# All four heads of two groups in eight turned by blocks, and row sums and routing ahead of the block transposes, in a post-norm decoder layer

## The chip, the cores and the metric

The kernel runs on one core of a Trainium2 chip. The metric is the device time of one execution in microseconds (us), the median of several runs. All data is float32. The engines are named as in the profile: PE does matrix products and transposes, PEld loads its weights, DVE, ACT and POOL work on vectors, and SP issues most DMA transfers. Each engine takes its instructions in the order in which they were written for it and waits on semaphores for the others.

## The reference

The layer takes `x` and `ctx` of shape 16 x 256 x 256 and a row of positions `frac` (16 x 256). It has three steps, each followed by a layer norm without weights. Cut to what matters here:

```
# 1. attention on fixed keys and values, 4 heads of 64
p = square(relu(q @ k.T)); x = norm(2*x + p @ v)

# 2. cross attention to ctx, 16 heads of 16, with a bias from positions
D      = clip(frac[:, None, :] - frac[:, :, None], -0.2, 0.2)
attn   = gamma * (Q @ K.T) / 4 + delta * (ap * max(D, 0) + an * min(D, 0))
probs  = softmax(attn, axis=-1)
x      = norm(x + (probs @ V) @ Wo.T + bo)

# 3. feed forward: the first of the largest of 8 gates chooses a low-rank addition
inner  = relu(x @ wi.T + wi_b + lora[top1](x))
x      = norm(x + inner @ wo.T + wo_b)
```

The change lies in step 2, in how `probs` is turned so that its key axis lies on the partitions, and in where parts of step 3 stand among it.

## The kernel before

Step 1 runs first, alone, to about 250 us. Then steps 2 and 3 run interleaved, in an order written out by hand (the whole program is under a manual schedule).

Step 2 is cut into 64 groups (`class Group`): one batch element and four of its heads, 256 queries by 256 keys. Group n belongs to batch element n // 4. The main loop at L1154 has one iteration per group and handles several at once: `now` is group n, `nxt` group n+1, `last` group n-1 and `older` group n-2. A group passes through these stages:

- `negative` (L636, POOL) and `positive` (L651, ACT) write the two halves of the position bias, the first into the tile `neg`, the second into four PSUM banks `ps_l`, one per head.
- `logits` (L659, PE) adds the products of queries and keys into the banks.
- `maxima` (L675, DVE) adds `neg` to the bank, keeps the sum in `neg` and takes each row's largest value.
- The rows are then made exponentials and turned, in one of two ways. In the first, `subtract` (L729, POOL or DVE) takes the maximum away, `turned` (L735, PE) transposes 128 x 128 pieces into PSUM, four per head, and `exps` (L749, ACT) writes their exponentials into the tile `pT`. In the second, `exp_rows` (L693, ACT) takes the exponential of the rows as they lie, with the maximum as bias, in two instructions per head; `blocks` (L701) transposes 32 x 32 blocks on DVE for two heads at once (into the tile `z`, or into the space of `kT`, which step 1 no longer needs) and writes them to DRAM (`away`); `fetch` (L722) reads them back by four DMAs, so that the blocks land in their places in `pT`.
- `attend` (L752, PE) multiplies `pT` by the values into the bank `av`, with a column of ones for the row sums. `keep` copies two groups' results out, and later pieces of the batch element (`gather`, `regroup`, `invert`, `spread`, `divide`, `project`) divide by the sums and apply the output weights.

Groups from number 14 on, but for the last two, are `direct` (L631): their heads 0 and 1 go the second way and their heads 2 and 3 the first.

Step 3 works on 512 tokens at a time, eight groups to such a block. Six of these blocks run inside the loop: with `part = (n - 15) % 8`, the iteration of part 0 transposes the block's rows (`turn`), part 1 computes the gates, part 2 chooses (`route`, a chain of small DVE instructions that ends in the tile `um`) and starts the inner product (`inner`, `turn_um`, `lora`), part 3 does its second half, and parts 4 to 7 do one quarter each of the outer product (`finish`, L994: `outer` on PE, then `add`, which adds the result to the rows on DVE and takes their statistics). In parts 5 and 7 the outer product uses the bank of the attends, and so no group is attended there; the group two before is attended one iteration later, together with the next one. So part 3's group is attended with part 4's in the iteration of part 6, and part 5's with part 6's in the next part 0.

In parts 2 and 3 (`halved`, L1215) the iteration has an order of its own. In the others, the block transposes of `now` are issued at L1302, after the row exponentials and ahead of `finish` (L1304); groups of parts 0 and 1 are `later` (L1210): their `blocks` and `fetch` wait for the next iteration. `fetch` of the other groups is issued at the start of the next iteration (L1189). All these DMAs go through SP's one queue, in order, together with those of the batch elements. PSUM space for transposes and small products comes from `tile_b`, three banks in turn.

Of the kernel before, what the change touches and what calls it, by code (L numbers as in the profile page):

```python
# [22 lines left out]
def tile_decoder_layer(ctx: ExitStack, tc: tile.TileContext, a: dict, out: bass.AP):  # L23
# [403 lines left out]
    if True:  # L427
# [199 lines left out]
        class Group:  # L627
            def __init__(self, batch, og):
                self.batch = batch
                self.o, self.i = divmod(og, 2)  # L630
                self.direct = DIRECT <= 4 * batch.b + og < 4 * B - 2  # L631

# [42 lines left out]
            def maxima(self):  # L675
# [3 lines left out]
                for g in range(4):  # L679
                    minus = self.direct and g < 2  # L680
                    for j in range(2):
# [10 lines left out]

            def exp_rows(self, g):  # L693

                for j in range(2):
                    nc.scalar.activation(  # L696
                        self.t[:, g, j, :], self.t[:, g, j, :], AF.Exp,
                        bias=self.mx[:, g, j : j + 1], scale=-1.0,
                    )

            def blocks(self):  # L701

                if self.i:
                    self.z = kT.rearrange("p n (c h q) -> p n c h q", c=2, q=32)
                else:
                    self.z = pm.tile([P, 4, 2, 4, 32], FP, tag="z", bufs=1, name="z")
                nc.vector.transpose(  # L707
                    self.z.rearrange("p n c h q -> p h c n q"),
                    self.t[:, 0:2].rearrange("p g j (c n k) -> p (g j) c n k", c=2, k=32),
                )  # L710
                self.away = drams.tile([P, 4, 4 * P // 2], FP, tag="blocks", name="away_z")
                nc.sync.dma_start(
                    out=self.away, in_=self.z.rearrange("p n c h q -> p n (c h q)")
                )

            def room(self):

                self.pT = pm.tile([P, 4, 2 * S], FP, tag="pT", name="pT")
                self.ps = {}
                self.pD = self.pT[:, 0:2].rearrange("p g (a c h q) -> p (g a) c h q", a=2, c=2, q=64)  # L720

            def fetch(self):  # L722
                for n in range(4):
                    nc.sync.dma_start(
                        out=self.pT[32 * n : 32 * n + 32, 0:2].rearrange("k g (a e) -> k (g a) e", a=2),
                        in_=self.away[:, n].rearrange("(r k) e -> k r e", k=32),
                    )

            def subtract(self, halves):  # L729
                for g, eng in ((2, nc.gpsimd),) if self.direct else zip((0, 2), halves):  # L730
                    rows = self.t[:, g : g + 2].rearrange("p g j k -> p (g j) k")
                    top = self.mx[:, g : g + 2].rearrange("p g j -> p (g j)").unsqueeze(2)
                    eng.tensor_tensor(rows, rows, top.to_broadcast([P, 4, S]), ALU.subtract)  # L733
# [18 lines left out]
            def attend(self):  # L752
# [4 lines left out]
                for k in range(2):  # L757
                    for g in range(4):
                        rhs = self.pT[:, g, k * S : (k + 1) * S]
                        to = batch.av[32 * g : 32 * g + 32, self.i * S : (self.i + 1) * S]  # L760
                        if self.direct and g < 2:
                            rhs = self.pD[:, :, k, g, :].rearrange("p r (j q) -> p j r q", j=2)
                            to = to.rearrange("p (j r q) -> p j r q", j=2, q=32)
# [18 lines left out]

        MADE, DIRECT = 5, 14
        batches = [Batch(b) for b in range(B)]
# [228 lines left out]
    with tc.manual_schedule():  # L1013
# [140 lines left out]
        for n in range(N + 2):  # L1154
# [53 lines left out]
            if now:  # L1208
                now.maxima()
                now.later = n >= FIRST and part in (0, 1)  # L1210
            if last and last.direct and last.later:
                last.blocks()
            if n == 29:
                by[NB] = scaling_of(rest_mv, newton(rest_mv, near_rest, 8), 8)
            if halved:  # L1215
                for g in range(2, 4) if last.direct else range(2):
                    last.turned(g)
                    last.exps(g)
                if part == 2:
                    ff.route()  # L1220
                if now.direct:
                    for g in range(2):
                        now.exp_rows(g)
                now.subtract((nc.gpsimd, nc.vector))
# [14 lines left out]
            else:  # L1239
# [7 lines left out]
                else:  # L1247
                    acts = "s0 s1 g s2 s3" if last.direct else "s0 e0 s1 e1 s2 s3"
                    if part != 0 or not ff:
                        acts += " x0 x1"  # L1250
                for act in acts.split():
# [9 lines left out]
                    elif act[0] == "x":  # L1261
                        if now:
                            now.exp_rows(g)
                    elif last:
# [17 lines left out]
            if ff and part == 0:  # L1282
# [3 lines left out]
                if now and now.direct:  # L1286
                    for g in range(2):
                        now.exp_rows(g)
            divided = batches[b - 2] if og == 0 and b >= 2 else None
# [9 lines left out]
            if done and not halved:  # L1299
                done.ready(newton(done.mv, done.near, 4))  # L1300
            if now and now.direct and not halved and not now.later:
                now.blocks()  # L1302
            if ff and part >= 4:
                ff.finish(part - 4, tile_v() if apart else None)  # L1304
            if last and (not last.direct or now and now.direct and not halved):
                for g in range(2, 4):
                    last.turned(g)
                    last.exps(g)
# [124 lines left out]
```

## Time and profile before

| what | value |
| --- | --- |
| median of 3 runs | 887.35 us (887.11 to 888.24) |
| the profiled execution | 887.49 us, its span 885.7 us |
| granted TensorE clock | 0.999 |
| DMA, over the span | 92.94 MB, 105 GB/s |
| L743, transposes on PE (heads turned the first way) | 640, 87.1 us busy, 277 ns each |
| L750, their exponentials on ACT | 160, 590 ns each |
| L696, exponentials of rows on ACT | 192, 498 ns each |
| L733, subtractions on POOL | 65, 1909 ns each |
| L707, block transposes on DVE | 24 into z at 1244 ns, 24 into kT at 1238 ns |
| DMA issues, blocks written to DRAM | 48 of 512 KB |
| DMA issues, blocks read back | 192 of 128 KB |

In a timeline, a line gives the start in us, the time in us, the engine, the source line, the operation, the tile written and the tiles read, the shapes, how many instructions were merged, and in brackets how long the engine sat idle before and what ended that. One float32 matmul shows as two records. Matmuls are pipelined: an instruction's own time is longer than the distance to the next, so eight transposes of 277 ns take about 1.04 us together.

### The profile page before, as it was taken

How to read it: one execution, taken by the hardware profiler on the slowest of the kernel's cores; microseconds unless marked ns; L12 is line 12 of the kernel's file. 1: busy time of each engine (PE TensorE's matmuls, PEld its weight loads, DVE VectorE, ACT ScalarE, POOL GpSimd, SP SyncE). 2: the span in 40 equal slices, each digit the busy share in tenths (PEclk: the TensorE clock that was granted, in tenths of full speed). 3: DMA queues.
4: the chain of work that ended last, by engine and by line, in shares of the span. 5: the costliest groups of instructions: out<-in, count | busy, mean ns of one | idle time of the engine just before them, and what ended most of it. 6: DMA issues, size and time to landing. Idle time of an engine off the chain costs nothing.

```text
span 885.7 us, 20853 instructions
## 1 busy us (share of the span) xinstructions
PE 862.4 (97%) x7708; PEld 513.1 (58%) x7708; DVE 693.3 (78%) x1975; ACT 577.0 (65%) x1012; POOL 466.6 (53%) x455
## 2 busy tenths in 40 slices
PE   8999999999999999999999999999999999999997
PEld 4334444444456776567547656754765675576655
DVE  6878899889779898769778877877887787777444
ACT  5766777777788788647747765774875577475111
POOL 1100223322479898656828765883976678374010
PEclk9999999999999999999999999999999999999999
DMA  5501101010001333454454536445453644642001
GB/s 139 159 1 43 54 24 44 31 49 1 8 8 48 99 98 110 139 162 149 158 155 150 158 129 184 151 155 168 138 164 133 193 151 135 181 149 102 28 7 41
DMA packets 70373, 92.94 MB, mean 105 GB/s; under 512 B 13824, under 2 KB 55296, under 8 KB 70272
## 3 DMA queue, kind: packets, MB, share of 16 engines
q1 hardware_dynamic: 69696, 91.35, 33.2%
q8 instruction: 61, 1.00, 0.5%
q14 instruction: 40, 0.33, 0.1%
q10 hardware_dynamic: 576, 0.26, 0.1%
HBM read 50.43 MB, written 39.58 MB: 102 GB/s over the span
## 4 chain that ended last, share of the span: by engine, by line
PE 44%; DVE 11%; issue 2%; POOL 1%; ACT 1%; DMA 0%; ACTq 0%; POOLq 0%; DVEq 0%
PE ps_l L945 9%; PE ps_b L978 6%; PE ps_l L664 5%; PE ps_v L764 5%; PE ps_b L743 4%; DVE neg L682 3%; PE ps_b L614 3%; PE ps_v L978 3%; PE ps_b L477 2%; PE ps_l L958 2%; DVE z L707 1%; PE ps_b L503 1%; PE ps_b L532 1%; POOL neg L733 1%; DVE dpos L547 1%
## 5 line engine op out<-in xcount | busy, mean ns | idle before, releaser
L682 DVE CUSTOM_DVE_ANT_0 neg<-ps_l,neg 128x256 f32<-128x256 f32 x512 | 181.5, 420 | 41.4 <-PE ps_l L664 38.3
L642 POOL TENSOR_SCALAR neg<-dneg,aneg,delta 128x512 f32<-128x512 f32 x252 | 198.9, 804 | 20.9 <-PE ps_b L743 10.0
L654 ACT ACTIVATE ps_l<-dpos,apos_d 128x512 f32<-128x512 f32 x256 | 172.2, 688 | 49.9 <-DVE mx L682 30.9
L354 DVE TENSOR_TENSOR pr<-pr 128x1024 f32<-128x1024 f32 x128 | 153.8, 1243 | 30.2 <-ACT pr L353 29.8
L733 POOL TENSOR_TENSOR neg<-neg,mx 128x1024 f32<-128x1024 f32 x65 | 124.0, 1909 | 85.4 <-DVE mx L682 84.3
L353 ACT ACTIVATE pr<-ps_a 128x1024 f32<-128x1024 f32 x128 | 125.0, 1026 | 53.0 <-PE ps_a L345 52.7
L345 PE MATMUL ps_a<-xnT,kT 64*64 64x512 f32 x1024 | 124.6, 593 | 1.0 <-ACT xnT L330 0.4
L364 PE MATMUL ps_v<-pr,vv 64*64 64x512 f32 x1024 | 122.7, 589 | 0.0
L945 PE MATMUL ps_l<-xt,wi 128*128 128x512 f32 x248 | 111.7, 596 | 0.2
L750 ACT ACTIVATE pT<-ps_b 128x512 f32<-128x512 f32 x160 | 87.4, 590 | 32.4 <-PE ps_b L743 30.9
L743 PE MATMUL ps_b<-ident,neg 128*128 128x128 f32 x640 | 87.1, 277 | 3.4 <-ACT pT L750 2.3
L743 PEld LDWEIGHTS ps_b<-ident,neg 128*128 128x128 f32 x640 | 71.5, 141 | 24.0 <-issue 6.2
L364 PEld LDWEIGHTS ps_v<-pr,vv 64*64 64x64 f32 x1024 | 45.0, 133 | 64.5 <-issue 54.6
L379 POOL TENSOR_TENSOR xt<-xt,half 128x512 f32<-128x512 f32 x15 | 19.1, 1274 | 119.8 <-ACT half L378 119.8
L419 POOL TENSOR_TENSOR hid<-hid,bo 128x256 f32<-128x256 f32 x32 | 43.6, 1366 | 71.8 <-ACT hid L251 71.8
L696 ACT ACTIVATE neg<-neg,mx 128x256 f32<-128x256 f32 x192 | 81.3, 498 | 0.0
L764 PE MATMUL ps_v<-pT,vaug 128*32 128x256 f32 x1024 | 74.3, 385 | 7.2 <-DVE x L991 6.0
L664 PE MATMUL ps_l<-kM,qT 32*64 32x256 f32 x2048 | 79.8, 388 | 0.0
L345 PEld LDWEIGHTS ps_a<-xnT,kT 64*64 64x64 f32 x1024 | 41.9, 133 | 65.3 <-issue 52.5
L945 PEld LDWEIGHTS ps_l<-xt,wi 128*128 128x128 f32 x248 | 45.6, 191 | 49.4 <-issue 44.6
L978 PE MATMUL ps_b<-wof,hT 128*128 128x256 f32 x304 | 68.4, 380 | 0.0
L524 POOL TENSOR_SCALAR kM<-keys,of_head 128x512 f32<-128x512 f32 x22 | 38.7, 1760 | 48.4 <-DVE keys L513 48.4
(137 smaller groups left out, 1183.3 us busy)
## 6 DMA issues: line engine op xcount, KB each, us to landing
pT<-away_z SPq DMA_DIRECT2D x192, 128.0 KB
away_z<-z SPq DMA_DIRECT2D x24, 512.0 KB
away_z<-kT SPq DMA_DIRECT2D x24, 512.0 KB
away_v<-raw SPq DMA_DIRECT2D x16, 512.0 KB
cT<-in_ctxT SPq DMA_DIRECT2D x16, 256.0 KB
v<-away_v SPq DMA_DIRECT2D x32, 128.0 KB
invs<-rows SPq DMA_DIRECT2D x16, 256.0 KB
x<-in_x SPq DMA_DIRECT2D x7, 512.0 KB
```

Of the source, the lines that this page charges most:

```text
L345: nc.tensor.matmul(sc[64 * k : 64 * k + 64, h, :], lhsT=kT[64 * h : 64 * h + 64, q, hf * P + 64 * k : hf * P + 64 * k + 64], rhs=self.xnT[ ...
L353: nc.scalar.activation(pr, sc, AF.Relu)
L354: nc.vector.tensor_tensor(pr, pr, pr, ALU.mult)
L364: nc.tensor.matmul(self.acc[k][64 * h : 64 * h + 64, :], lhsT=vv[64 * k : 64 * k + 64, hf, 64 * q : 64 * q + 64], rhs=pr[64 * k : 64 * k + ...
L642: nc.gpsimd.tensor_scalar(self.neg[:, g], self.batch.dneg, aneg[:, h : h + 1], delta, ALU.mult, ALU.mult,)
L654: nc.scalar.activation(banks[g], self.batch.dpos.rearrange("p j k -> p (j k)"), AF.Copy, scale=apos_d[:, h : h + 1],)
L664: nc.tensor.matmul(banks[g][64 * h : 64 * h + 64, j * S : (j + 1) * S], lhsT=self.batch.qT[rows, self.o, j * P + 64 * h : j * P + 64 * h + ...
L682: nc.vector.tensor_tensor_reduce(out=self.t[:, g, j, :], in0=banks[g][:, j * S : (j + 1) * S], in1=self.neg[:, g, j, :], scale=-1.0 if min ...
L733: eng.tensor_tensor(rows, rows, top.to_broadcast([P, 4, S]), ALU.subtract)
L743: nc.tensor.transpose(ps[:, k * S + j * P : k * S + (j + 1) * P], self.t[:, g, j, k * P : (k + 1) * P], ident,)
L945: nc.tensor.matmul(self.banks[g], lhsT=wi[:, c, f * P : (f + 1) * P], rhs=self.xT[:, c, :], start=(c == 0), stop=False,)
L978: nc.tensor.matmul(ps[:, 0:C], lhsT=self.hT[f][:, j * P : (j + 1) * P], rhs=wof[:, f, :], start=(f == 0), stop=(f == FC - 1),)
```

## The change

A direct group now has a number of pairs of heads that go the second way: 1 as before, or 2. It is 2 for groups of part 3 and part 4, from n = 18 to n = 58: eleven groups. Such a group has no `subtract`, no `turned` and no `exps`; `exp_rows` covers its four heads, `maxima` takes negative maxima for all four, `blocks` does two transposes (the first into `z`, the second into `kT`) and two writes, and `fetch` reads pieces of twice the size: four DMAs of 256 KB instead of 128 KB. In DRAM the blocks of the two pairs lie interleaved: a write of one pair goes to 512 runs of 1 KB instead of 128 runs of 4 KB, and a read takes runs of 2 KB instead of 1 KB.

Two orders change for all turns: `ff.route()` stands ahead of `last.blocks()` in part 2 (it stood inside the `halved` branch, after the transposes of the group before), and `ff.finish` stands ahead of `now.blocks()` in parts 4 to 7.

```
             def __init__(self, batch, og):
                 self.batch = batch
                 self.o, self.i = divmod(og, 2)
-                self.direct = DIRECT <= 4 * batch.b + og < 4 * B - 2
+                n = 4 * batch.b + og
+                self.direct = DIRECT <= n < 4 * B - 2
+                self.pairs = 0
+                if self.direct:
+                    self.pairs = 2 if DIRECT < n < 4 * B - 5 and (n - DIRECT - 1) % 8 in WHOLE else 1
...
-                    minus = self.direct and g < 2
+                    minus = g < 2 * self.pairs
...
-            def exp_rows(self, g):
-
-                for j in range(2):
...
+            def exp_rows(self):
+
+                for g in range(2 * self.pairs):
+                    for j in range(2):
...
             def blocks(self):
 
-                if self.i:
-                    self.z = kT.rearrange("p n (c h q) -> p n c h q", c=2, q=32)
-                else:
-                    self.z = pm.tile([P, 4, 2, 4, 32], FP, tag="z", bufs=1, name="z")
-                nc.vector.transpose(
-                    self.z.rearrange("p n c h q -> p h c n q"),
-                    self.t[:, 0:2].rearrange("p g j (c n k) -> p (g j) c n k", c=2, k=32),
+                self.away = drams.tile(
+                    [P, 4, self.pairs, 2 * P], FP, tag=f"blocks{self.pairs}", name="away_z"
                 )
-                self.away = drams.tile([P, 4, 4 * P // 2], FP, tag="blocks", name="away_z")
-                nc.sync.dma_start(
-                    out=self.away, in_=self.z.rearrange("p n c h q -> p n (c h q)")
-                )
+                for m in range(self.pairs):
+                    if m or self.pairs == 1 and self.i:
+                        z = kT.rearrange("p n (c h q) -> p n c h q", c=2, q=32)
+                    else:
+                        z = pm.tile([P, 4, 2, 4, 32], FP, tag="z", bufs=1, name="z")
+                    nc.vector.transpose(
+                        z.rearrange("p n c h q -> p h c n q"),
+                        self.t[:, 2 * m : 2 * m + 2].rearrange(
+                            "p g j (c n k) -> p (g j) c n k", c=2, k=32
+                        ),
+                    )
+                    nc.sync.dma_start(
+                        out=self.away[:, :, m], in_=z.rearrange("p n c h q -> p n (c h q)")
+                    )
...
             def fetch(self):
                 for n in range(4):
                     nc.sync.dma_start(
-                        out=self.pT[32 * n : 32 * n + 32, 0:2].rearrange("k g (a e) -> k (g a) e", a=2),
-                        in_=self.away[:, n].rearrange("(r k) e -> k r e", k=32),
+                        out=self.turned_in[32 * n : 32 * n + 32],
+                        in_=self.away[:, n].rearrange("(r k) m e -> k r (m e)", k=32),
                     )
 
             def subtract(self, halves):
-                for g, eng in ((2, nc.gpsimd),) if self.direct else zip((0, 2), halves):
+                for g, eng in ((2, nc.gpsimd),)[: 2 - self.pairs] if self.direct else zip((0, 2), halves):
...
-                        if self.direct and g < 2:
-                            rhs = self.pD[:, :, k, g, :].rearrange("p r (j q) -> p j r q", j=2)
+                        if g < 2 * self.pairs:
+                            rhs = self.pD[:, :, g // 2, k, g % 2, :].rearrange("p r (j q) -> p j r q", j=2)
...
-        MADE, DIRECT = 5, 14
+        MADE, DIRECT, WHOLE = 5, 14, (3, 4)
...
+            if ff and part == 2:
+                ff.route()
             if last and last.direct and last.later:
                 last.blocks()
...
-                if part == 2:
-                    ff.route()
...
+            if ff and part >= 4:
+                ff.finish(part - 4, tile_v() if apart else None)
             if now and now.direct and not halved and not now.later:
                 now.blocks()
-            if ff and part >= 4:
-                ff.finish(part - 4, tile_v() if apart else None)
             if last and (not last.direct or now and now.direct and not halved):
-                for g in range(2, 4):
+                for g in range(2 * max(last.pairs, 1), 4):
                     last.turned(g)
                     last.exps(g)
```

`room` lays out `pT` for one or two pairs (`turned_in`, `pD`) accordingly.

## The prediction

> **What bounds the kernel now.** I read the page first, then the timelines of all engines over one turn of eight groups, the DMA queue's waits, and the landing events of the transfers. Span first:
>
> ```profile
> span 885.7 us, 20853 instructions
> PE 862.4 (97%) x7708; PEld 513.1 (58%) x7708; DVE 693.3 (78%) x1975; ACT 577.0 (65%) x1012; POOL 466.6 (53%) x455
> ```
>
> PE is nearly always busy, so one would take PE work for the bound. The chain of waits repeats every eight groups; its L872 (the gates, part 1) starts at 509.39, 586.00, 662.62 and 739.24: one turn is 76.62 us, and there are six. I call the group at n = 15+8k "part 0", the next part 1, and so on, as the code's `part`. In the turn I read, the logits (L664) of parts 1 to 7 start at 583.09, 589.75, 604.28, 617.90, 627.16, 634.46, 643.63, and of the next part 0 at 650.93. PE from part 4 on:
>
> ```profile
> 622.26 3.62 PE L978 MATMUL ps_b<-wof,hT 128*128 128x256 f32 x16
> 625.72 1.04 PE L743 MATMUL ps_b<-ident,neg 128*128 128x128 f32 x8
> ...
> 633.50 1.04 PE L743 MATMUL ps_b<-ident,neg 128*128 128x128 f32 x8
> 634.46 1.12 PE L664 MATMUL ps_l<-kM,qT 32*64 32x256 f32 x32
> 635.51 1.93 PE L764 MATMUL ps_v<-pT,vaug 128*32 128x256 f32 x32
> 637.38 1.99 PE L614 MATMUL ps_b<-wo,oT 128*128 128x256 f32 x8
> 639.21 3.62 PE L978 MATMUL ps_b<-wof,hT 128*128 128x256 f32 x16
> 642.66 1.04 PE L743 MATMUL ps_b<-ident,neg 128*128 128x128 f32 x8
> ...
> 652.83 2.65 PE L764 MATMUL ps_v<-pT,vaug 128*32 128x256 f32 x32 [0.78 <-DVE x L991]
> ```
>
> The attends (L764) of part 0 show PE waiting: 0.78 us before them, and 2.65 us where the same 32 records at 635.51 took 1.93. So PE has about 1.6 us of slack there, and something else sets the end of that stretch. On DVE:
>
> ```profile
> 624.97 1.25 DVE L707 STREAM_TRANSPOSE kT<-neg 128x1024 f32<-128x1024 f32 x1 [0.72 <-ACT neg L696]
> 626.14 0.38 DVE L991 TENSOR_TENSOR x<-x,ps_b 128x256 f32<-128x256 f32 x1
> ...
> 633.75 1.25 DVE L707 STREAM_TRANSPOSE z<-neg 128x1024 f32<-128x1024 f32 x1 [1.91 <-ACT neg L696]
> ...
> 644.91 0.42 DVE L682 CUSTOM_DVE_ANT_0 neg<-ps_l,neg 128x256 f32<-128x256 f32 x1 [0.35 <-PE ps_l L664]
> ```
>
> From the maxima of part 7 (644.91) DVE runs without a gap through reciprocal, keys, dpos and the Newton steps to 651.2; ACT's x2 rows (651.34 to 653.32) and the exponentials (to 654.38) hang on that, and then the attend's end. So from 644.91 the turn is DVE then ACT; from part 0's attends to part 4 it is PE. What delays 644.91 delays the whole turn.
>
> **What the change does, part by part.** Eleven groups become "whole": parts 3 and 4 of the first five turns, part 3 of the sixth.
>
> PE loses 8 transposes in each: 1.04 us less the overlap, 0.97 to 1.04 (the L743 rows at 625.72 and 633.50). At part 2, routing stands ahead of the block transpose: PE now waits 0.53 us for `um` (the row at 597.83); routing takes DVE 594.98 to 598.19 = 3.21, and moved to 593.82 it is done at 597.03, before PE's L945 ends at 597.3, so the 0.53 goes. Routing's two PE transposes, now ahead of part 1's, need only the gates' copy of part 1. If nothing else bound, 11 × 1.04 + 6 × 0.53 = 14.6 us.
>
> POOL loses 11 subtractions of 1.9 us (off the path: it idled 7.34 before the one of part 3). ACT per whole group gains four exponentials (four take 1.69, so +1.6) and loses two L750 (1.08). DVE gains one transpose, 1.17 from start to start. SP gains one write, 0.33 to 0.41 to issue, on a queue that mostly waits.
>
> Costed at nothing, with the cover: in part 3 ACT idles 5.93 before L967 and DVE 2.40 before L971 (615.14), more than 1.6 and 1.17; were that cover gone, each would add what exceeds it. Part 3's attend comes only at part 6 (`apart` skips part 5), so its 1 MB fetch, issued near 618 to 620, has 14 us. Part 1's block, put 3.2 us later, is fetched only at 606.38 anyway: SP first waits there for the raw copy. Part 7's block goes behind the row sums, 1.06 later; its fetch landed at 659.67 and would land at 660.8; the attend at 660.83 waits for exponentials until 661.5. Less than 0.6 of cover is left; beyond that it costs one for one, and part 6's block and fetch, also later, have 1.5 left.
>
> Not hidden is part 4. By rows, in the same clock:
> 1. The outer product (L978) ended at 625.72; 0.53 earlier now: 625.19.
> 2. The row sums go first: add 0.26 later (the lag of L682 behind L664 at 584.14/584.40), 1.06 to the end of the statistics (626.14 to 627.20): 626.51. ACT's eight exponentials end at 625.98 (after the 0.53 shift, 622.78 + 8 × 0.40), so they do not bind.
> 3. Two transposes, 1.17 and 1.25: 628.93, where before it was 626.22. Part 5's maxima, queued behind them, start at 628.85 instead of 628.44; through L654 and the exponentials part 5's block comes at 634.2 and part 6's maxima at 635.3 (before: 635.91). No loss there.
> 4. SP writes the blocks, then fetches. Before:
>
> ```profile
> 626.24 0.33 SPq L712 DMA_DIRECT2D away_z<-kT  x1
> 629.22 1.80 SPq L724 DMA_DIRECT2D pT<-away_z  x4
> ```
>
> The write landed 2.85 after its issue and released the fetch 0.13 later; the fourth piece of the fetch landed at 633.60, 4.38 after the first issue; the attend of part 4, second half of the row at 635.51, read it at 636.45, with 2.85 of slack. Now the write is two DMAs whose DRAM side is 512 pieces of 1 KB, and the fetch is 1 MB, not 512 KB. Write: at least 2.62 (the commonest landing of the 4 KB form), at most 4.21 (a 512 KB out<-x in 1 KB pieces, at 810.35); I take 2.96 (the same store at 862.17, nothing beside it), the nearest in form. Fetch: at least 4.38 (half the bytes), at most 7.43 (eight pieces of 128 KB in part 3, 606.38 to 613.81, in a crowd); the four landings of 128 KB were 0.56 apart and issue allowed 0.46, so doubling the pieces costs up to four times 0.56 = 2.2 and no less than nothing. I take 1.0, a transfer partly issue-bound: 5.4. Landing: 628.95 + 2.96 + 0.13 + 5.4 = 637.4.
> 5. PE gets to this attend at 634.6 (logits at 632.6, held by L654; part 3's attend; 1.85 earlier than before). It then waits 2.8 us for DMA, a wait that was not there. Behind it on PE stand project (L614), the outer product, part 5's transposes and part 7's logits; for project DVE's `hid` waits, for the outer product its row sums, and for these, by the new order, part 6's block, and then part 7's maxima.
> 6. From landing L: attend L + 1.05, project 1.83, outer product 3.45, add 0.26, statistics 1.06, transpose 1.17: part 7's maxima start at L + 8.82. Before: 644.91. Each turn thus changes by L − 636.1: at 637.44, **+1.34**. If L came earlier, DVE's own queue would hold maxima at 643.8, a floor of −1.1.
>
> The sixth turn has no whole part 4, and there the new order helps:
>
> ```profile
> 788.23 1.93 PE L764 MATMUL ps_v<-pT,vaug 128*32 128x256 f32 x32 [1.63 <-DVE x L991]
> ```
>
> That 1.63 goes when the sums precede the block; with the 0.53 and 1.04 it could be 3.2, but part 4's one-pair block there goes behind the sums (626.51 to 627.7 in the clock above, 1.5 later), its fetch lands at 633.60 + 1.5 + 152.8 (the logits of part 5 are at 779.91) = 787.9, and that attend stood at 789.2, so 1.3 is sure; I take 1.6.
>
> Sum: 5 × 1.34 − 1.6 = +5.1. The profiled execution took 887.49 (span 885.7 and 1.8 around it), the median of runs 887.35; on the median this is **892.5 us**.
>
> [...] The trace has a 512 KB write at 2.62 and four 128 KB fetches at 4.38. [...]
>
> **Rivals.**
> *Fetch in time.* If L ≤ 635.0 the floor −1.1 holds in five turns: −5.5 − 1.6 gives 880.3; with DVE no bound at all, 14.6 gives 872.7. For it: PE's 97%. Against: write plus fetch would need 6.0 us, and the lowest rows sum to 7.1; only an earlier end of DVE's blocks could make it up.
> *A wash.* L between 636.1 and 636.8, the low ends of both rows: 0 to +0.7 a turn, −1.6 at the end: 885.8 to 889.1, say 887.5. The change then moves work from PE to the transfer and buys nothing.
> *The transfer is worse.* At both high ends L = 640.7, +4.6 a turn: 908.8; halfway between the taken and the high, +3: 901. It decides from L of 638.5. For it: DMA ran at 1.05 of its engines' time from 610 to 614 and out<-x there landed after 6.5 us, with part 3's second block now added. Against: from 627 the queue is nearly empty.
> That the change doesn't do what it says I exclude: in the built order the eleven groups have two block transposes each and eight transposes less on PE.
>
> **How the numbers follow.** Forecast (888.9 to 898, around 892.5) 0.42; transfer worse, 0.15; wash 0.15; fetch in time 0.28, because six of my links are lags of 0.2 to 0.5 and one unnoticed earlier release frees a us per turn. A change under 0.2% (1.8 us) can't be told from none here. Faster 0.28, same 0.15, slower 0.57. Range 881 to 902: half of the fast case and half of the worst case fall outside.
>
> **What would show it.** Right: in the first five turns PE idles 2 to 3 us before part 4's attend, the one x32 row after part 6's logits, released by pT's DMA; L743 is gone after parts 4's and 5's outer products; the 0.53 before `um` is gone; a turn lasts about 78 us, the sixth under 76. Wrong: attends of part 6 back to back and turns of 75.5; or the wait at part 0 (exponentials after the x2 rows) growing by itself.

## The result, and the profile after

The changed kernel takes 928.49 us in the median of four runs (925.08 to 930.47), the kernel before 887.31 beside it: a ratio of 1.0458, 95% interval 1.0426 to 1.049. It is slower, as forecast, but by 41.2 us and not by 5.1. The page of the changed kernel, whose profiled execution took 925.08 us:

```profile
span 923.3 us, 20672 instructions
PE 865.5 (94%) x7620; PEld 509.6 (55%) x7620; DVE 708.5 (77%) x1986; ACT 582.9 (63%) x1034; POOL 444.9 (48%) x444
...
PEclk9999999999999999989998999899899989999999
```

PE has 88 instructions less than before and is yet busy 3.1 us longer. The third line gives the granted clock in 40 slices: five slices in the interleaved part are below 9, one in each of the first five turns (a turn is eight groups). The PE timeline of one of them, from part 4's outer product on (start, duration, line; in brackets the idle time before and what ended it):

```profile
647.50 0.60 PE L464 MATMUL ps_b<-ident,hid 128*128 128x128 f32 x4
...
654.70 1.12 PE L668 MATMUL ps_l<-kM,qT 32*64 32x256 f32 x32
655.75 1.07 PE L779 MATMUL ps_v<-pT,vaug 128*32 128x256 f32 x16
663.38 1.94 PE L779 MATMUL ps_v<-pT,vaug 128*32 128x256 f32 x16 [6.56 <-DMA pT<-away_z]
665.24 2.54 PE L614 MATMUL ps_b<-wo,oT 128*128 128x256 f32 x8
667.62 3.62 PE L993 MATMUL ps_b<-wof,hT 128*128 128x256 f32 x16
...
691.08 1.07 PE L779 MATMUL ps_v<-pT,vaug 128*32 128x256 f32 x16 [1.74 <-DMA pT<-away_z]
```

The two rows of L779 at 655.75 and 663.38 are part 3's and part 4's attends: before, one row of 32 at 635.51 without a gap. Between them PE stands still for 6.56 us. The row behind the wait then takes 1.94 where the same 16 records take 1.07, and L614 takes 2.54 instead of 1.99. The last row is part 7's attend in the next part 1; it too waits now, 1.74 in this turn and 0.9 or less in the other four. The windows of the same turn, whose columns are length, busy time and count of PE, PEld, DVE, ACT and POOL, the granted clock, the DMA engines' share, and GB/s:

```profile
645.00:655.20 10.20, 10.03 (x93) 8.00 (x98) 7.95 (x27) 7.62 (x17) 7.21 (x8) 1.00 0.97 235
655.20:664.00 8.80, 2.24 (x48) 1.03 (x36) 4.62 (x20) 7.31 (x15) 8.14 (x9) 0.75 0.64 182
664.00:668.00 4.00, 4.00 (x25) 2.63 (x16) 0.87 (x2) 0.00 (x0) 0.00 (x0) 0.70 0.44 133
668.00:691.00 23.00, 20.97 (x212) 15.39 (x210) 18.08 (x65) 16.14 (x32) 15.98 (x16) 1.00 0.42 139
```

From 645 to 655, when part 4's write has to go out, the DMA engines are busy for 97% of the time. In the stretch of the wait and just behind it the clock is at 0.75 and 0.70: the clock's own record has 0.5 for 6.8 us there, from 2.75 us after the start of the wait to 3.02 after its end, and once in each of the other four turns for 6.8 to 10.2 us. The transfer itself, in the list of the chain that ended last (start, us, what):

```profile
644.21 3.45 PE ps_b L993 x16
651.09 4.40 DMA away_z<-kT
658.24 5.00 DMA pT<-away_z
```

The write lands 4.40 after its issue; the first piece of the fetch is issued at 655.64, the last at 658.24, and the last lands at 663.24, 12.15 after the write's issue.

Where the turn's time went, this turn (84.71 us from attend to attend of part 1, 606.37 to 691.08) against the same one before (76.62): to the end of part 4's outer product -0.45; from there to part 6's logits -1.54, for the two rows of eight transposes that are gone; part 6's attends +7.62, of which 6.56 is the wait; project to part 7's logits +0.55, since project begins at half the clock (L614's 2.54 for 1.99); part 7's attend +1.81; the rest +0.1. The sum is +8.09. The turns differ: from one start of the gates to the next, the first five are 6.1, 6.6, 8.7, 7.7 and 6.8 us longer than before (35.9 of the 37.6 us between the two profiled spans), and the sixth is 1.0 longer.

### The profile page after: what moved, and what is told of

Same layout as the page of the kernel before. It is cut to its first block, busy times and chain, and to the rows that moved or that the text cites. A ratio compares the mean times of both kernels' runs of the same rounds, so it can differ in the third digit from the quotient of the medians.

```text
span 923.3 us, 20672 instructions
## 1 busy us (share of the span) xinstructions
PE 865.5 (94%) x7620; PEld 509.6 (55%) x7620; DVE 708.5 (77%) x1986; ACT 582.9 (63%) x1034; POOL 444.9 (48%) x444
## 4 chain that ended last, share of the span: by engine, by line
PE 38%; DMA 9%; DVE 8%; issue 2%; SPq 2%; ACT 1%; DVEq 0%; ACTq 0%
PE ps_l L960 9%; PE ps_b L993 7%; DMA pT<-away_z 5%; PE ps_v L779 4%; PE ps_l L668 4%; PE ps_b L614 4%; DMA away_z<-kT 3%; PE ps_b L758 2%; DVE neg L686 2%; PE ps_l L973 2%; SPq L739 2%; PE ps_b L532 1%; DVE kT L716 1%; PE ps_b L503 1%; PE ps_b L477 1%
## 5 line engine op out<-in xcount | busy, mean ns | idle before, releaser
L748 POOL TENSOR_TENSOR neg<-neg,mx 128x1024 f32<-128x1024 f32 x54 | 103.1, 1910 | 46.9 <-DVE mx L686 40.2
L779 PE MATMUL ps_v<-pT,vaug 128*32 128x256 f32 x1024 | 79.8, 404 | 40.6 <-DMA pT<-away_z 36.9
L765 ACT ACTIVATE pT<-ps_b 128x512 f32<-128x512 f32 x138 | 75.6, 590 | 65.6 <-PE ps_b L758 62.5
L701 ACT ACTIVATE neg<-neg,mx 128x256 f32<-128x256 f32 x236 | 98.9, 498 | 0.0
L779 PEld LDWEIGHTS ps_v<-pT,vaug 128*32 128x32 f32 x1024 | 30.5, 112 | 88.6 <-issue 53.7
L758 PE MATMUL ps_b<-ident,neg 128*128 128x128 f32 x552 | 75.5, 277 | 3.0 <-ACT pT L765 2.3
L758 PEld LDWEIGHTS ps_b<-ident,neg 128*128 128x128 f32 x552 | 61.5, 141 | 20.4 <-issue 5.5
```

What stands on the lines that cost most here:

```text
L758: nc.tensor.transpose(ps[:, k * S + j * P : k * S + (j + 1) * P], self.t[:, g, j, k * P : (k + 1) * P], ident,)
L779: nc.tensor.matmul(to, lhsT=batch.va[:, k, self.head(g), :], rhs=rhs, start=(k == 0), stop=(k == 1),)
```

## The experiments

Each run was timed beside the kernel before (887.7 to 888.3 us in these comparisons).

**The orders alone.** No group is whole; both new orders stay.

```
-        MADE, DIRECT, WHOLE = 5, 14, (3, 4)
+        MADE, DIRECT, WHOLE = 5, 14, ()
```

> No group is whole here; only the two orders are changed (routing and row sums ahead of the block transposes). Theory (the loss is the wait of part 4's attend for the 1 MB of a whole group, and what follows on it): near the time before, 885 to 892 us, no PE idle of over 1.5 us before the attends of part 6, granted clock 0.998 or more; the wait before part 1's attend of part 7, whose block is 1.1 us later, may cost up to 1 us in each of six turns. Rival (the new orders make the loss, since all blocks of parts 4 to 7 start later): 905 us or more. The 0.53 before um should still be there if POOL's subtraction slows routing's L916 wherever it stands beside it.

897.68 us, ratio 1.0106 (1.0077 to 1.0134): the orders by themselves cost 9.4 us, more than the theory expected and less than its rival. Two later runs split them. The first keeps the new order of the routing alone, the second that of the row sums.

```
+            if now and now.direct and not halved and not now.later:
+                now.blocks()
             if ff and part >= 4:
                 ff.finish(part - 4, tile_v() if apart else None)
-            if now and now.direct and not halved and not now.later:
-                now.blocks()
```

> No whole groups, the old order in the finish, the routing of part 2 ahead of the block transposes (new). Theory: the row sums ahead of the transposes are what made 897.7 of the two orders, by part 7's later write, so the routing alone is worth between -2 and +1: 885 to 889. The rival, that the routing delays the transposes that stand behind it: 893 to 898.

> No whole groups, the old order in the routing, the row sums ahead of the block transposes at parts 4 to 7 (new). Theory: part 7's attend waits 1.4 to 1.9 us for its fetch in most turns, 895 to 899. The rival (routing): 886 to 889.

The routing: 888.17 us, 1.0001 (0.9992 to 1.0009). The row sums: 894.6 us, 1.0073 (1.0052 to 1.0095). So the loss is the row sums', as far as the runs can tell, and the routing moved nothing. PE's waits by line and releaser (us in all, times, longest), first the kernel before, then the row sums first:

```profile
PE ps_v L764 <- DVE x L991: 6.0, 6, 1.6
PE ps_b L919 <- DVE um L909: 2.6, 5, 0.5
```

```profile
PE ps_v L779 <- DMA pT<-away_z: 6.3, 7, 1.7
PE ps_v L779 <- issue: 3.6, 2, 2.0
```

The waits for the row sums' result (`x`) are gone but for one of 0.6, as they should be, and waits for the fetch have come in their place. ("issue" means that the profile shows nothing that released PE; the two waits stand at attends where the run with both orders waits for the fetch.) Waits for the last exponentials there grew too, from 0.4 to 3.2. Together PE's waits before attends grew from 6.9 to 13.7 us in the two profiled executions. One turn of that kernel, SP and then PE, shows why:

```profile
654.52 0.34 SPq L722 DMA_DIRECT2D away_z<-z  x1
657.92 1.74 SPq L739 DMA_DIRECT2D pT<-away_z  x4
...
663.54 1.07 PE L779 MATMUL ps_v<-pT,vaug 128*32 128x256 f32 x16 [1.68 <-DMA pT<-away_z]
```

Part 7's write stands behind its row sums: it is issued 7.34 ahead of the time at which PE could start this attend (663.54 less 1.68), before 8.26 (652.50 against 660.76). And the fetch is issued 3.40 after the write, where before that was 2.94 (652.50 to 655.44).

Why the routing brought nothing, in the DVE and POOL timeline of the changed kernel:

```profile
615.83 1.89 POOL L748 TENSOR_TENSOR neg<-neg,mx 128x1024 f32<-128x1024 f32 x1 [0.52 <-DVE lg L908]
616.04 1.73 DVE L916 TENSOR_TENSOR hot<-lg,top 128x32 f32<-128x32 f32 x1
```

and of the kernel before:

```profile
594.05 1.90 POOL L733 TENSOR_TENSOR neg<-neg,mx 128x1024 f32<-128x1024 f32 x1 [0.49 <-DVE mx L682]
595.39 0.60 DVE L901 TENSOR_TENSOR hot<-lg,top 128x32 f32<-128x32 f32 x1
```

The comparison of 32 columns takes 1.73 or 0.60, and in both kernels it ends 0.04 to 0.05 after POOL's subtraction does. The same in the run with the routing alone: POOL from 595.22 to 597.11, DVE to 597.16. Issued earlier, it only stands longer. Three pairs of ends are all that this rests on; what joins the two operations the traces do not show.

**The whole groups alone.** The old orders, parts 3 and 4 whole.

> Parts 3 and 4 are whole, both orders as before. Theory: part 4's second block ends about 1.4 us earlier (it still waits for eight exponentials), so the wait before its attend falls from 6.6 to about 5 us, and part 7's fetch is in time again: 905 to 915 us. Rival (the orders make the loss): under 895. Rival (the volume of DMA alone makes it, wherever the block stands): unchanged, 922 or more.

919.15 us, 1.0348 (1.0331 to 1.0365): 9.3 less than the changed kernel, which is again the price of the orders, but above the expected 905 to 915. The transfer is what makes most of the loss:

```profile
654.10 1.07 PE L779 MATMUL ps_v<-pT,vaug 128*32 128x256 f32 x16 [1.60 <-DVE x L1006]
659.87 1.93 PE L779 MATMUL ps_v<-pT,vaug 128*32 128x256 f32 x16 [4.70 <-DMA pT<-away_z]
```

**One of the two parts whole.** Part 3 with the old orders, then part 4 with the new ones.

```
-        MADE, DIRECT, WHOLE = 5, 14, (3, 4)
+        MADE, DIRECT, WHOLE = 5, 14, (3,)
```

> Only part 3 is whole, both orders as before. Theory: part 3's fetch has over 10 us until its attend at part 6, so nothing waits, PE loses 1.04 us in each of six turns and DVE's maxima of parts 5 to 7 move up with it: 880 to 884 us, faster than both kernels. Rival (more DMA traffic or DVE time costs in itself): 888 or more.

> Only part 4 is whole, both new orders. Theory (two causes: part 4's own second block and 1 MB, and part 3's 1 MB in the queue ahead of it): part 4's write lands in about 3 us instead of 3.6 to 5.1, the attend of part 4 still waits, about 4 us instead of 6.6: 908 to 918. Rival (part 4's own transfer is all of it): 923 or more. Rival (part 3 is all of it): under 900, as with the orders alone.

Part 3 alone: 887.1 us, 0.9986 (0.9977 to 0.9996), 0.1% less, where 880 to 884 was expected. Part 4 alone: 922.56 us, 1.04 (1.0377 to 1.0422), with waits of 4.5 to 5.2 before its attend in all five turns and long rows behind them (1.93 or 1.94 for 16 records in four turns, 1.51 for 12 in the other, where 12 take 1.06 elsewhere), at a mean granted clock of 0.978. Its second write landed after 3.65 to 3.86, not after the expected 3, and its fetch took 7.0 to 7.6, although no megabyte of part 3 runs ahead of it here. So part 4's own transfer makes most of the loss; part 3 as a whole group adds some 6 us more.

**The wait kept, the clock kept.** The changed kernel with 48 transposes of the identity on PE ahead of part 4's attend; nothing reads them.

```
                     groups[n - 3].attend()
+                if older.pairs == 2 and part == 6:
+                    ps = tile_b()
+                    for j in range(48):
+                        nc.tensor.transpose(ps[:, j % 4 * P : (j % 4 + 1) * P], ident, ident)
                 older.attend()
```

> The changed kernel with 48 transposes of the identity on PE ahead of part 4's attend where it is whole (five times), about 6.2 us of PE work that nothing reads. Theory (PE's idle lets the granted clock fall to half for some 7 us, and the attend and project after it run slower: 1.07 became 1.94 and 1.99 became 2.54): the clock stays at 1.0 there, about 1.4 us less in each of five turns, 919 to 924 us. Rival (the clock costs nothing, the wait alone does): 927 or more.

917.82 us, 1.0324 (1.0298 to 1.035): doing more work on PE makes the kernel 10.7 us faster. The PE timeline of that run:

```profile
648.21 5.46 PE L1203 MATMUL ps_b<-ident 128*128 128x128 f32 x48
654.79 1.07 PE L779 MATMUL ps_v<-pT,vaug 128*32 128x256 f32 x16 [1.12 <-DMA pT<-away_z]
655.79 1.99 PE L614 MATMUL ps_b<-wo,oT 128*128 128x256 f32 x8
```

The wait is as long as before (5.46 of filling and 1.12 of idling), but behind it the attend takes 1.07 and L614 1.99, as in the stretches where the clock's record is 1.0, and the mean granted clock is 0.996, the changed kernel's 0.979. PE's waits for the fetch sum to 9.6 in this run, and five fills of 5.46 make 27.3; together 36.9, the changed kernel's own total. So the transfer's lateness is not touched, and the 10.7 us are the clock's. They are more than the 1.4 a turn, 7 in all, that was expected from the turn shown. The record of the changed kernel agrees: of its five falls 3.0 to 6.2 us each lie behind the end of the wait, 23.7 in all, and at half speed that costs up to 11.9 us (an estimate).

**What makes the transfer late: four versions.** The write goes to runs of 1 KB (as in the change) or 4 KB (each pair of heads has its own area in DRAM); and the fetch waits for both writes as a whole, or its first half goes when the first write has landed. The second version:

```
-                    [P, 4, self.pairs, 2 * P], FP, tag=f"blocks{self.pairs}", name="away_z"
+                    [P, self.pairs, 4, 2 * P], FP, tag=f"blocks{self.pairs}", name="away_z"
...
-                for n in range(4):
-                    nc.sync.dma_start(
-                        out=self.turned_in[32 * n : 32 * n + 32],
-                        in_=self.away[:, n].rearrange("(r k) m e -> k r (m e)", k=32),
-                    )
+                for m in range(self.pairs):
+                    for n in range(4):
+                        nc.sync.dma_start(
+                            out=self.turned_in[32 * n : 32 * n + 32, :, 256 * m : 256 * m + 256],
+                            in_=self.away[:, m, n].rearrange("(r k) e -> k r e", k=32),
+                        )
```

> The changed kernel, but each pair of a whole group has its own part of DRAM: writes go in runs of 4 KB again, and the fetch is eight DMAs of 128 KB in runs of 1 KB. The bytes are the same. Theory (the write of part 4's second block takes 3.6 to 5.1 us because part 3's 1 MB fetch and the loads behind it still fill the queue): within 6 us of the changed kernel, 922 to 932. Rival (the 1 KB runs of the write make it long): the write falls to about 2.7 and the turn by 1 to 2 us, 917 to 922.

901.7 us, 1.0171 (1.0146 to 1.0196). The theory that part 3's megabyte makes the write long fell: the second write now lands after 2.8 us in four turns and 3.45 in one. But this run changed three things at once: the runs of the write, those of the read (1 KB instead of 2 KB), and the start of the fetch. Two more take them apart: the changed layout with the divided fetch, and this layout with the second pair fetched first, so that nothing can go before the second write is in.

```
-                for m in range(self.pairs):
+                for m in reversed(range(self.pairs)):
```

> The changed kernel, its store of the block transposes laid out as in it (runs of 1 KB in the write), but the fetch of each pair in eight transfers of 128 KB with runs of 1 KB, the first four of which need the first of the two writes alone. Theory W (the write's 1 KB runs are what made 928): the write still lands after 3.6 us or more, the last fetch after 11 us or more from the write's issue, 918 to 928. Theory R (the 2 KB reads, and that all of them waited for both writes): 899 to 908, the clock falling in at most two turns.

> The version with an area of its own for each pair (901.7), with the second pair's heads fetched first, so that nothing is fetched before the second write has landed. If the early start of the first half made the gain: 906 to 918, one wait of 4 us or more before part 4's attend, and the clock falls in most turns. If the length of the runs alone made it: 899 to 904.

| write's runs | fetch waits for both writes | first half goes with the first |
| --- | --- | --- |
| 1 KB | 928.49 (the change) | 909.68, 1.0238 (1.0213 to 1.0264) |
| 4 KB | 924.85, 1.0403 (1.0371 to 1.0434) | 901.7 |

(The read's runs are 2 KB in the first field and 1 KB in the others.) The last two expectations missed by their sizes: the early start of the first half is worth 18.8 or 23.2 us, the longer runs of the write only 3.6 or 8.0. The 18.8 and the 3.6 include the change of the read's runs, and the intervals of 928.49 and 924.85 overlap, so 3.6 is not clear of the scatter. The 23.2 includes that PE needs first the half that is fetched last there. Between the two versions of the right column only the layout in DRAM differs: with 1 KB runs the second write lands after 3.6 to 3.8. The fetch of the megabyte takes 6.7 to 8.1 in all three new versions. SP's and PE's timeline with both cures:

```profile
634.30 0.33 SPq L722 DMA_DIRECT2D away_z<-kT  x1
636.00 3.84 SPq L740 DMA_DIRECT2D pT<-away_z  x8
...
640.78 0.63 PE L780 MATMUL ps_v<-pT,vaug 128*32 128x256 f32 x4 [0.76 <-DMA pT<-away_z]
644.22 1.92 PE L780 MATMUL ps_v<-pT,vaug 128*32 128x256 f32 x12 [2.81 <-DMA pT<-away_z]
```

and with long runs but a late start:

```profile
648.20 0.33 SPq L722 DMA_DIRECT2D away_z<-kT  x1
651.16 4.50 SPq L740 DMA_DIRECT2D pT<-away_z  x8
...
658.65 2.15 PE L780 MATMUL ps_v<-pT,vaug 128*32 128x256 f32 x16 [4.72 <-DMA pT<-away_z]
```

In the first, the fetch begins 1.70 after the second write's issue, in the second 2.96 after it. The first has two shorter waits with work between them, and the rows behind are long in one turn of five, the one shown (1.92 for the 12 records, 1.06 in the other four); the second has one long wait, and the 16 records behind it take 2.14 or 2.15 in all five.

**Making part 3 alone pay.** Part 3's megabyte and the next loads of `cT` and `frow` stand on SP ahead of part 4's write of one pair, which then landed after 4.2 to 6.05 us instead of 2.6 to 2.85. Here part 4's loads are held back to the end of part 5:

```
             for extra in pieces(n)[2]:
-                if extra:
+                if extra and n > FIRST and (n - FIRST) % 8 == 4:
+                    held.append(extra)
+                elif extra:
                     extra()
...
+            while held and (n - FIRST) % 8 == 5:
+                held.pop(0)()
```

> Only part 3 whole, old orders, and the two loads of a later batch element (384 KB) that stand on SP between part 3's fetch and part 4's write go to the end of part 5's iteration. Theory (in the kernel with part 3 whole, part 4's 512 KB write takes 4.5 to 6.0 us where it took 2.6 before, since the queue holds part 3's 1 MB and these loads; its attend then waits 1.2 us): the write falls below 4 us, the wait goes, about 1 us less in each of five turns: 880 to 885. Rival (part 3's 1 MB alone fills the queue): 886 to 889, unchanged.

883.59 us, 0.9959 (0.9944 to 0.9973): 0.4% faster than the kernel before, which is small but clear of the scatter. The place of the loads is worth some 3 of these 4.3 us, going by the run without it: part 4's write now lands after 2.6 to 4.4. (The profiled execution was the slowest of the six, 886.81, with one wait of 2.66 left.) Two other edits brought nothing. The first is part 3 whole, without the late loads, with the row sums first in the sixth turn alone:

> Only part 3 whole, old orders, but in the sixth turn the row sums stand ahead of the block transposes. Theory (in the sixth turn no query product stands behind part 5's logits, PE waits over 1.6 us for part 5's row sums, and the clock then falls to half for 3.4 us): the wait and the half clock there go, 1.5 to 2.5 us less than with part 3 whole alone: 884 to 886. Rival (the sixth turn's attend then waits for DMA or DVE instead): no change, 887.

887.05 us, 0.9996 (0.998 to 1.0013): the rival's value; in the sixth turn the attend now waits 1.58 for the fetch. The second is the late loads with an area for each pair:

> Only part 3 whole, old orders, late loads of part 4 (883.6), with an area of its own for each pair of heads and fetches of 128 KB: 881 to 884 if part 3's long-run transfer also clears the way for part 4's write of one pair; unchanged, 883 to 885, if part 3's transfer was hidden in any case.

883.39 us, 0.9954 (0.994 to 0.9968): not to be told from 883.59; part 3's transfer was hidden.

**Can both parts pay?** Old orders, both cures of the transfer, late loads; then the same with the row sums first in part 4, or between the two transposes, or first in part 5.

> Parts 3 and 4 as whole groups, with the old order in the finish and the routing, an area of its own for each pair and fetches of 128 KB, and part 4's next loads held back to the end of part 5's: 886 to 893 if the transfer is what made 919 of the old orders and its cure is worth what it was in the changed kernel (901.7 less some 9 for the orders, less 4 for the loads). A rival: the old order issues the write later, so the waits stay above 3 us and the clock falls again: above 900. Below 883 only if part 4's first product block costs less than its wait.

> As the version with both parts whole, old orders, areas of their own and late loads (892.3), but with the row sums ahead of both transposes in part 4 alone. The waits for the row sums' result there (1.6 to 2.1 us in six places) go; the writes are issued some 1.8 us later, and the fetch, which was in time in all but two turns, is then late by what slack it lacked: 886 to 893; above 893 if it had no slack at all and the clock falls with the wait.

> As that version (892.3), but with the row sums between the two transposes in parts 3 and 4: the row sums wait for one transpose, as in the kernel before, so the waits of 1.6 to 2.1 us for their result go; the first half's write is not moved, the second is issued some 1 us later: 880 to 887. The rival, that the second half then lands late: 889 to 894.

> As the version with both parts whole, old orders, areas of their own and late loads (892.3), but with the row sums ahead of the transpose in part 5 alone, where VectorE stands idle for 1.9 us before that transpose and TensorE waits 1.5 to 2.1 us for the sum, six times, 10.5 in all. If that wait is the price that is left: 882 to 887, and no wait of more than 0.3 us for the row sums' result before part 4's attend. If the fetch is late right behind it: 888 to 893.

In this order: 892.3 us, 1.0048 (1.0036 to 1.006); 899.32, 1.0126 (1.011 to 1.0142); 892.88, 1.0042 (1.0027 to 1.0057); 892.2, 1.0037 (1.0018 to 1.0056). None is faster than before. The two in the middle were aimed at a wait that does not arise in part 4: in the first of the four versions PE's timeline has it at 563.88, where the attends of parts 3 and 4 need the bank that part 5's row sums read. (Why the second version is 7 us slower than the first stays open.) The last run moved just those row sums, and PE's waits show what became of it, first without the move, then with it:

```profile
PE ps_v L780 <- DVE x L1007: 14.5, 11, 2.1
PE ps_v L780 <- DMA pT<-away_z: 4.7, 3, 2.3
```

```profile
PE ps_v L780 <- DMA pT<-away_z: 13.0, 10, 2.9
PE ps_v L780 <- DVE x L1007: 4.3, 5, 1.1
```

10.2 us of waits for the sums went, 8.3 came back as waits for the fetch, and the time did not move. The transfer stood right behind, as the run's rival said.

## Why the prediction was too low

The place and the wait were right: PE waits before part 4's attend for the DMA of `pT` in each of five turns, and the rivals "a wash" and "fetch in time" are both out. The rival "the transfer is worse" comes nearest, but even its upper end, 908.8, is 20 below. Two steps failed: step 4, the length of the transfer, was too short by 3.7 us a turn, and the clock's fall behind the wait was missing from step 6. Step by step, in the turn read above:

1. *The outer product of part 4 ends 0.53 earlier, since the `um` gap goes.* Wrong: the gap before the row at 619.61 is still 0.52 (1.11 in two other turns), as one of routing's operations ends with POOL's subtraction in both orders (0.04 to 0.05 after it). The step took routing's 3.21 us as a fixed length; that operation went from 0.60 to 1.73 when moved. The run with this order alone: 888.17, no change. (The 0.45 that the turn shown does gain up to here lies in its first attend, which takes 1.35 to the next row instead of 1.79.)
2. and 3. *Row sums, then two transposes, 3.74 us.* Right. In the DVE timeline:

```profile
647.70 0.42 DVE L1006 TENSOR_TENSOR x<-x,ps_b 128x256 f32<-128x256 f32 x1 [1.67 <-PE ps_b L993]
...
648.71 1.23 DVE L716 STREAM_TRANSPOSE z<-neg 128x1024 f32<-128x1024 f32 x1
649.86 1.20 DVE L716 STREAM_TRANSPOSE kT<-neg 128x1024 f32<-128x1024 f32 x1
```

From the outer product's end at 647.50 to the second transpose's end at 651.06 it is 3.56.

4. *Write 2.96, release 0.13, fetch 5.4: 8.49 in all.* This is the step that failed. It measured 4.40 + 0.14 + 7.60, and 12.15 from issue to landing. In the five turns the write took 3.6 to 5.1 and the fetch 7.2 to 7.6, in part beyond the high ends (4.21 and 7.43). The value chosen for the write was that of a store with "nothing beside it", and "from 627 the queue is nearly empty" was read from the kernel before, where the DMA engines were busy for 36% of the stretch from 625 to 634. In the changed kernel they are busy for 97% from 645 to 655, with part 3's own megabyte, fetched from 642.35 to 650.07, and the loads. But that traffic is not most of the error: with part 4 alone whole the write still took 3.65 to 3.86 and the fetch 7.0 to 7.6. For the write the runs of 1 KB count, since runs of 4 KB bring it to 2.8 in four turns of five; the traffic may explain the two turns with 4.40 and 5.08. The doubled fetch was priced at +1.0, and it costs 3.2 over the old 4.38: its four pieces of 256 KB land 1.2 to 1.6 apart, where those of 128 KB landed 0.56 apart. Part 5's write of 512 KB, issued at 658.77 while the fetch runs, may lengthen it; no run separates that. And the structure went unseen: with one fetch for both pairs, half of the data waits for a write that it does not need. Letting that half go early is worth 18.8 to 23.2 us in the four versions, the clock's part included. With 12.15 for the 8.49 the prediction's own sum would give +5.0 a turn and 910.8 in all (an estimate); the rest of the way to 928.49 lies in what follows.
5. *PE waits 2.8.* 6.56 here, 5.8 to 6.7 in the five turns: the 2.8 plus the 3.7 of step 4.
6. *From the landing on, 8.82 to part 7's maxima, each turn +1.34.* This failed too: the stretch was costed at full clock. PE idles 6.56, the clock's record falls to 0.5 at 2.75 into that wait, and PE pays on the work behind it: 10.7 us in all by the run with the fill, a term that no step had.

*Costed at nothing: part 7's block, with 0.6 of cover.* Wrong too: the write and the fetch of part 7 land later than the step added up, as its row sums put both of them behind, and the attend waits 1.74 in the turn shown. With the row sums' order alone the cost is 6.5 us, with both orders 9.4; whether these differ by more than the runs scatter stays open, as their intervals overlap.

*Sixth turn, -1.6.* It did not come: the 1.63 for `x` at the attend is gone, and in its place PE waits 1.77 for part 4's fetch there. That turn is 1.0 us longer than before.

The terms, as far as runs separate them: of 41.2 us, the cures of the transfer (first half early, long runs) give back 26.8, and with it nearly all of the clock's 10.7; the orders are 9.4; some 5 are left, which is what both parts whole with old orders and all cures still cost (892.3 against 887.7). That remainder did not go in any of three further versions, and its cause stays open. The saved PE work is real (1.54 in this turn), but it only shortens PE's way to a wait for a transfer that cannot come sooner.

## What to carry to other kernels

A round trip by DRAM must be priced for its own size and length of runs and in the traffic of the changed kernel, not from a transfer of half the size in the gap that the old one left (8.49 was taken here, 12.15 measured); ask for each piece of the fetch which write it really needs, and let it go with that. A wait on PE can have a second price: behind the waits of 5.8 to 6.7 us here the clock's record stayed at 0.5 for 3.0 to 6.2, and it shows as longer rows of the same instruction (1.94 for 1.07); without it the kernel was 10.7 us faster. And an order that removes a wait for one result delays every transfer that is issued behind it: with the row sums first, in parts 4 to 7 or in part 5 alone, waits for the sums became waits for a fetch.

## What the runs showed of the hardware

The clock. In the changed kernel the record of 0.5 begins 2.3 to 5.1 us after the start of PE's waits of 5.8 to 6.7 us, still inside them, and lasts 6.83 us in four turns and 10.24 in one; between these five it stands at 1.0 for 75.09 us twice and 78.51 twice. All these lengths are within 0.01 of whole multiples of 3.413, a third of the 10.24. Shorter waits were not safe, going by the rows right behind them. Where the record is 1.0, the 16 records of an attend take 1.07 and L614 takes 1.99. Behind a wait of 2.66, in the version with part 3 whole and late loads, the 16 took 1.94; behind one of 2.92 in the last run, 1.73; behind one of 2.00 in the run with both orders, 1.50, and L614 then 3.21. Others near 2 us passed: behind one of 1.98, in the run with the row sums first, it was 1.07 and 1.99. In the version with the row sums first in part 4, two waits of 2.11 had 32 records of 4.07 and 3.82 behind them, and a third of 2.11 had 20 of 1.49, the same as a wait of 1.60 in the version with the row sums between the transposes. Behind 1.86 and 1.80, with both orders, the 16 took 1.07. Of two waits close together, 1.45 and 1.65 in the version with 1 KB runs and the first half early were followed by 1.92 for 12 records, 1.66 and 1.75 in another of its turns by 1.06. So these runs give no one length of wait that divides the two.

SP's issue. The four pieces of part 4's fetch take SP 3.03 us in the turn shown, 2.58 in the last and some 1.75 in the other three; two of them were issued 1.75 apart (656.02 and 657.77), beside a packet of 1.40 us at 655.95 on the queue for instructions. That is a coincidence in time, seen in other places of the trace (an issue of 1.68 at 542.92 beside a packet of 1.35 at 542.88, one of 1.60 at 560.17 beside one of 1.24 at 560.16); no run separates it. It does not explain the late fetch, which took 7.2, 7.4 and 7.6 in the three turns without it.
